# Cached keys gathered already turned, with their rotation partners, instead of rotated in rows and transposed by TensorE

## The chip, the cores and the metric

The kernel runs on one core of a Trainium2 chip. The metric is the device time of one execution in microseconds (us); lower is better. Engines are named as the profile names them: PE is TensorE (PEld its weight loads), DVE is VectorE, ACT is ScalarE, POOL is GpSimd, and SP is SyncE, which here only issues transfers.

## What is computed

The reference is one decoder layer in float32: self-attention over a selected cache, layer norm, cross-attention, layer norm, a linear layer with low-rank experts, layer norm. There are 2048 tokens (32 rows of 64) of 512 features. The change lies in the self-attention alone, which is cut here to what matters:

```python
q = (x @ wq.T).reshape(b, l, 32, 128)           # 32 query heads
k = (x @ wk.T).reshape(b, l, 8, 128)            # 8 key/value groups
v = (x @ wv.T).reshape(b, l, 8, 128)
q, k = apply_rope(q, cos, sin), apply_rope(k, cos, sin)   # one angle per feature pair
k_sel = k_cache[block_idx].reshape(-1, 8, 128)  # 16 blocks of 32 cached keys
v_sel = v_cache[block_idx].reshape(-1, 8, 128)
k_full = concatenate([k_sel, k[0]])             # 512 cached keys and 64 new ones
v_full = concatenate([v_sel, v[0]])
scores = einsum('bhld,bhtd->bhlt', q, repeat(k_full, 4)) / sqrt(128)
out = einsum('bhlt,bhtd->bhld', softmax(scores), repeat(v_full, 4))
return out.reshape(b, l, 4096) @ wo.T
```

All tokens have the same position, so one rotation by one set of angles serves every query and every new key. The kernel never rotates the queries: it applies the inverse rotation to the cached keys instead, and multiplies the new keys by cos^2 + sin^2. A pair of neighbouring features (e, o) of a cached key becomes (e cos + o sin, o cos - e sin).

## The kernel before

**Units.** The self-attention is a loop over 128 units `n`: 8 groups, in each 4 blocks of 512 tokens, in each 4 heads. `r = n % 16` is the place of a unit in its group, `b = n // 4` its block, `h` its head. A unit treats its 512 tokens in four tiles of 128. For each tile PE makes 128x576 scores against `kT` (features on the partitions, 576 keys) into one of two PSUM rooms (`sc`, two buffers); DVE takes the row maximum (L884); ACT does the exponential with the sum (L890); DVE inverts the sum (L919); ACT or DVE scales (L921, L923); DVE turns 32x32 blocks (L931). When all four tiles of a unit are turned, `move` (L943) rearranges them with 16 transfers, issued by SP, into `pT`, and two units later PE multiplies by the values (`values`, L951). For units 0, 1, 2 one quarter of these transfers is issued by POOL instead.

**Queries and projections.** Between the tiles PE computes the queries of the next block and the output projection of a block before, by a seven-product scheme; in blocks 8 to 31 the queries (`qd`, L1170) use a deeper form of it, for which POOL loads operands (L1147, `load_tokens`) and adds up the results (`post`, L1185 to L1191). POOL also makes the sums of weights and tokens for these schemes (`wo_sums` L262 to L265, `outer_sums` L1132, `output_sums` L351 to L355).

**Keys of the next group.** While group `g` runs, the keys of `g + 1` are made ready. `gather_keys` fetches at r = 4 to 7 one quarter of the cached keys each (128 rows of 512 bytes, an indirect transfer, L774), after DVE has made its row numbers (L789); `gather_values` does the same for the values in the same units. From r = 8 on, `rotate` turns the pairs in two halves, with four DVE and two POOL instructions each (L808 to L813); `new_keys` makes the 64 new keys and values on PE at r = 8; `cached_keys` transposes the rotated rows with four PE instructions (L848) into a PSUM bank at r = 10, and two ACT instructions (L851) scale them into `kT`. Group 0 does all that in an opening stage, from rows that arrive early.

**Order.** In the opening stage the order of all five engines is the order of the code (`manual_schedule`). In the loop that holds for PE, DVE, ACT and POOL; SP's order is made by the scheduler, which takes an instruction when what it needs is ready. An engine runs its queue in order, and a waiting instruction holds up all behind it. Loads that can wait are put into a list, `spread`, from which POOL issues one at certain places of a unit.

**Tokens.** The token features of block `b + 2` are loaded in four pieces of 256 KB (`load_pieces`, L122), up to block 7.

Of the kernel before, what the change touches and what calls it, by code (L numbers as in the profile page):

```python
# [28 lines left out]
NKEY = NSEL + SEQ  # L29
# [23 lines left out]
def decoder_layer(  # L53
# [13 lines left out]
    wvT: bass.AP,  # L67
    woT: bass.AP,
    k_cache: bass.AP,
    v_cache: bass.AP,  # L70
    block_idx: bass.AP,
    xwq: bass.AP,
    xbq: bass.AP,
    xwkv: bass.AP,
# [633 lines left out]
    with ExitStack() as ph:  # L708
# [64 lines left out]
        def gather(g, dst, src, t):  # L773
            nc.gpsimd.indirect_dma_start(  # L774
                out=dst[:, t, :], out_offset=None, in_=src,
                in_offset=bass.IndirectOffsetOnAxis(ap=rows_cur[g][:, t : t + 1], axis=0),
            )

        def gather_keys(g, t):
            if t == 0:  # L780
                rows_cur[g] = kv.tile([P, NKT], I32, tag="row", name=f"row{g}")
                kn_cur[g] = kv.tile([P, NKT, HD], F32, tag="kn", name=f"kn{g}", bufs=1)
                kr_cur[g] = kv.tile([P, NKT, HD], F32, tag="kr", name=f"kr{g}", bufs=1)
                vs[g] = kv.tile([P, NKC, HD], F32, tag="v", name=f"v{g}")
            if g == 0:
                if t == 0:
                    nc.vector.tensor_scalar(rows_cur[g], row_f, 0.0, None, ALU.add)
            else:
                nc.vector.tensor_scalar(  # L789
                    rows_cur[g][:, t : t + 1], row_f[:, t : t + 1], float(g), None, ALU.add  # L790
                )
            gather(g, kn_cur[g], k_rows, t)

        def gather_values(g, t):
            gather(g, vs[g], v_rows, t)

        def rotate(g, t0=0, t1=NKT):

# [21 lines left out]
        def new_keys(g):  # L820

            wk, wv = wkv_cur.pop(g)
            kTs[g] = kv.tile([P, NKEY], F32, tag="kT", name=f"kT{g}")
# [41 lines left out]
        def scores(n, i):  # L867
            scores_first(n, i)
            scores_last(n, i)
# [325 lines left out]
        for dst, src in ((cs2, cos2), (sn2, sin2)):  # L1195
            nc.sync.dma_start(out=dst, in_=src)
        nrm2 = kc.tile([P, 1], F32, name="nrm2")
        for dst, src in ((bk, xbk), (bv, xbv)):
            nc.sync.dma_start(out=dst, in_=src)
        load_group(0, nc.sync)  # L1200
# [10 lines left out]
        for i in range(2):  # L1211
# [2 lines left out]
                xTs[0].rearrange("p c (j k) -> p c j k", j=TPB)[:, :, :, : SEQ // TPB],  # L1214
            )
        nc.vector.tensor_tensor(t[1], q[0, 1], q[0, 0], sub)
        nc.vector.tensor_tensor(wq0[7], wq0[1], wq0[5], sub)
        nc.vector.tensor_tensor(wq0[5], wq0[5], wq0[4], ALU.add)
        nc.vector.tensor_tensor(t[2], q[1, 1], t[1], sub)
        nc.vector.tensor_tensor(wq0[6], wq0[5], wq0[1], sub)  # L1220
        rotate(0, 0, NKT // 2)
        nc.vector.tensor_tensor(wq0[3], wq0[2], wq0[6], sub)
        nc.vector.tensor_tensor(nrm2, cs2, cs2, ALU.mult)
        nc.vector.tensor_tensor(sn2, sn2, sn2, ALU.mult)
        nc.vector.tensor_tensor(nrm2, nrm2, sn2, ALU.add)
# [58 lines left out]
        for n in range(N):  # L1284
            b, h = divmod(n, REP)
            g, r = units[n][0], n % PER
            if r == REP + 2 and g + 1 < NKV:
                load_group(g + 1, nc.gpsimd)
            if r in gathers and g + 1 < NKV:
                gather_keys(g + 1, gathers[r])  # L1290
            if 0 < n <= PER:
                b2, j = divmod(n - 1, TPB)
                args = dict(out=acc[b2][:, j, :], in_=rows(x, b2)[:, j, :])
# [116 lines left out]
            if n < (PLAIN - 2) * REP or n >= N - REP:  # L1410
                def leaf(place):
                    for part in leaves.pop(4 * (n - 1) + place, ()):
                        part()
                    if 4 * (n - 1) + place not in full:
                        run_some(spread, 1)

                scores(n, 0)
                step(0)
                leaf(0)
                spare_bank()  # L1420
                run_some(rotations, 1)
                scores(n, 1)
                if n - 1 in short:
                    move(n - 1, (3,), nc.gpsimd)
                if n == N - 1:
                    kv_sums()
                if n >= 2:
                    values(n - 2, 0, first_half)
                leaf(1)
                step(1)  # L1430
                scores(n, 2)
                step(2)
                if h == 1 and b and wo_sums:
# [12 lines left out]
                step(3)  # L1446
                spare_bank()
            else:
                assert not leaves
                k = REP * h  # L1450
                filled = h == 1 and b + 1 >= PLAIN and b + 1 < NB
                scores(n, 0)
                project()
                run_some(rotations, 1)
                scores_first(n, 1, lambda: query(k))
                scores_last(n, 1)
                if n - 1 in short:
                    move(n - 1, (3,), nc.gpsimd)
                if h != REP - 1:
                    values(n - 2, 0, first_half)  # L1460
                    query(k + 1)
                run_some(rotations, 1)
                scores(n, 2)
                if h == REP - 1:
                    query(k + 1)
                if h != 1:
                    project()
                if h == REP - 1:
                    values(n - 2, 0, first_half)
                elif filled:  # L1470
                    query(6)
                spare_bank()
                if r in gathers and g + 1 < NKV:
                    gather_values(g + 1, gathers[r])
                scores_first(n, 3, None if filled else lambda: query(k + 2))
# [794 lines left out]
```

## Time and profile before

| what | value |
|---|---|
| time, median of 3 runs | 2975.94 us (2974.57 to 2977.52) |
| the profiled execution's own time | 2976.36 us |
| its span in the profile | 2974.6 us, so 1.8 us lie around it |
| granted TensorE clock | 0.999 |
| PE busy | 2953.1 us, 99% of the span |
| DVE, ACT, POOL busy | 64%, 50%, 57% |
| DMA engines | six to seven tenths busy in the first half |
| chain that ended last | PE 96%, DVE 2%, DMA 1%, ACT 1% |
| self-attention loop | units start at about 21 us (unit 0), 41 (2), 61 (4), 85 (6), 115 (8), then some 14 us each |

The times of instructions come from one profiled execution on the only core. A busy PE in this profile includes the pipelined ends of its matmuls, so the chain that ended last, which gives each instruction the time by which it moved the end, is the better view for what a PE instruction costs.

### The profile page before, as it was taken

The page shows a single profiled execution, that of the slowest core. Times are in us where ns is not written, and L with a number is a line of the kernel's source. Part 1 is how long each engine was busy: PE and PEld are TensorE (multiplying, and loading weights), DVE is VectorE, ACT ScalarE, POOL GpSimd, SP SyncE. Part 2 cuts the span into 40 slices and gives each one's busy share as a digit, 9 for nine tenths or more (in the row PEclk, how much of TensorE's full clock was granted, in tenths as well). Part 3 has the DMA queues.
Part 4 walks back from the last instruction along what each step waited for, and adds up shares of the span by engine and source line. Part 5 has one row for each costly group of instructions (what it writes and reads, how often), then busy time and mean ns, then how long its engine had stood idle before and what let it go on. Part 6 is the DMA issues. An engine that isn't in the chain of part 4 may idle for free.

```text
span 2974.6 us, 49393 instructions
## 1 busy us (share of the span) xinstructions
PE 2953.1 (99%) x17152; PEld 2336.0 (79%) x17152; DVE 1907.8 (64%) x3569; ACT 1480.7 (50%) x3303; POOL 1699.4 (57%) x1698
## 2 busy tenths in 40 slices
PE   9999999999999999999999999999999999999998
PEld 6677777777777777777777768999999999999965
DVE  6666666666666666666666665636666665666676
ACT  4444455555555455455555552334555555555564
POOL 5666554564564564664663534658577577567532
PEclk9999999999999999999999999999999999999999
DMA  6677656666566666566565554766455545445420
GB/s 170 185 197 194 173 143 157 159 162 158 156 164 155 156 167 158 153 168 155 155 169 154 136 132 148 255 235 214 160 185 184 169 166 194 166 162 184 137 82 36
DMA packets 220262, 487.31 MB, mean 164 GB/s; under 512 B 52912, under 2 KB 87856, under 8 KB 211824
## 3 DMA queue, kind: packets, MB, share of 16 engines
q1 hardware_dynamic: 177872, 341.51, 39.6%
q0 software_dynamic: 40752, 140.94, 16.8%
q8 instruction: 139, 2.28, 0.3%
q10 hardware_dynamic: 1392, 1.70, 0.2%
q14 instruction: 107, 0.88, 0.1%
HBM read 264.27 MB, written 46.66 MB: 105 GB/s over the span
## 4 chain that ended last, share of the span: by engine, by line
PE 96%; DVE 2%; DMA 1%; ACT 1%; SPq 0%; issue 0%; POOL 0%; POOLq 0%; DVEq 0%
PE po L951 17%; PE s L877 17%; PE qd L1170 9%; PE sx L1766 2%; PE pox L1849 2%; PE qx_0x L519 2%; PE qx_1x L519 2%; PE qx_2x L519 2%; PE qx_3x L519 2%; PE wx_3y L380 1%; PE wx_2y L380 1%; PE wx_0y L380 1%; PE w_3y L380 1%; PE w_2y L380 1%; PE w_1y L380 1%; PE w_0y L380 1%
## 5 line engine op out<-in xcount | busy, mean ns | idle before, releaser
L877 PE MATMUL s<-kT,qT 128*128 128x288 f32 x2048 | 581.3, 408 | 0.0
L890 ACT ACTIVATE p<-s,nmax 128x576 f32<-128x576 f32 x512 | 378.3, 739 | 358.6 <-DVE nmax L884 333.7
L951 PE MATMUL po<-pT,v 128*128 128x512 f32 (+1 forms) x1280 | 549.5, 603 | 4.8 <-DMA pT<-T 3.5
L884 DVE TENSOR_REDUCE nmax<-s 128x1 f32<-128x576 f32 x512 | 384.4, 751 | 246.8 <-PE s L877 241.3
L921 ACT ACTIVATE p<-p,den 128x576 f32<-128x576 f32 x416 | 322.7, 776 | 358.7 <-DVE den L919 354.8
L877 PEld LDWEIGHTS s<-kT,qT 128*128 128x128 f32 x2048 | 371.0, 190 | 107.2 <-issue 31.1
L931 DVE STREAM_TRANSPOSE T<-p 128x576 f32<-128x576 f32 x512 | 395.5, 772 | 48.1 <-ACT p L921 40.8
L1147 POOL DMA_DIRECT2D tq<-tq x336 | 182.9, 547 | 416.9 <-PE qd L1170 406.2
L951 PEld LDWEIGHTS po<-pT,v 128*128 128x128 f32 (+1 forms) x1280 | 204.2, 189 | 191.0 <-issue 178.1
L1170 PEld LDWEIGHTS qd<-tq,wq 128*128 128x128 f32 x1344 | 174.5, 191 | 48.4 <-issue 32.3
L1170 PE MATMUL qd<-tq,wq 128*128 128x128 f32 x1344 | 179.0, 276 | 0.0
L1170 PEld LDWEIGHTS qd<-tq,xT 128*128 128x128 f32 x1008 | 136.3, 191 | 51.9 <-issue 23.0
L1170 PE MATMUL qd<-tq,xT 128*128 128x128 f32 x1008 | 142.1, 277 | 0.0
L1869 ACT ACTIVATE oTx<-pox,bv 128x128 f32<-128x128 f32 x248 | 71.3, 490 | 128.6 <-PE pox L1849 128.6
L919 DVE RECIPROCAL den<-den 128x1 f32<-128x1 f32 x512 | 78.4, 153 | 72.1 <-ACT p L890 70.4
L1191 POOL TENSOR_TENSOR qT<-qT,tx 128x512 f32<-128x512 f32 x72 | 89.2, 1265 | 61.7 <-DVE qT L1179 61.6
L351 POOL TENSOR_TENSOR sox<-oTx,oTx 128x512 f32<-128x512 f32 x31 | 39.3, 1268 | 148.5 <-DVE oTx L1871 144.7
L1798 ACT ACTIVATE exps<-exps,denx 128x64 f32<-128x64 f32 x480 | 121.1, 338 | 0.0
L561 POOL TENSOR_TENSOR qTx<-d_in 128x512 f32<-128x512 f32 x68 | 85.3, 1276 | 34.5 <-ACT d_in L537 26.7
L890 ACT ACTIVATION_READ_ACCUMULATOR p<-s,nmax 128x1 f32 x512 | 99.5, 194 | 0.0
L1177 ACT COPY tx<-qd 128x512 f32<-128x512 f32 x96 | 56.1, 584 | 67.8 <-PE qd L1170 62.6
L561 POOL TENSOR_TENSOR qTx<-d 128x512 f32<-128x512 f32 x60 | 75.1, 1274 | 24.6 <-ACT d L537 23.2
(630 smaller groups left out, 6350.5 us busy)
## 6 DMA issues: line engine op xcount, KB each, us to landing
pT<-T SPq DMA_DIRECT2D x1016, 80.0 KB
pT<-T SPq DMA_DIRECT2D x1008, 64.0 KB
xT<-tl SPq DMA_DIRECT2D x28, 1792.0 KB
tq<-tq POOLq DMA_DIRECT2D x168, 256.0 KB
tlb<-tl SPq DMA_DIRECT2D x28, 1344.0 KB
tq<-tq POOLq DMA_DIRECT2D x168, 192.0 KB
kv_room<-kv SPq DMA_DIRECT2D x32, 512.0 KB
pTx<-Tx SPq DMA_DIRECT2D x256, 64.0 KB
```

What stands on the lines that cost most here:

```text
L380: nc.tensor.matmul(self.banks[b][:, m, :], self.left[i][:, k, m * P : (m + 1) * P], self.right[i][:, k, :], start=(first and m + k == 0), ...
L519: nc.tensor.matmul(o[:, j, :], self.left[s][:, j, LEFT[i], :], self.right[s][:, j, RIGHT[i], :], start=(first and j == 0), stop=(j == len( ...
L561: nc.gpsimd.tensor_tensor(self.q[:, :, i, :, v, :], x.rearrange("p (o u) n -> p o u n", o=2), y.rearrange("p (o u) n -> p o u n", o=2), AL ...
L877: nc.tensor.matmul(s[:, a, :HALF], query_block(n, i), kTs[g][:, a * HALF : (a + 1) * HALF], start=True, stop=True,)
L884: nc.vector.tensor_reduce(nmax, s[:, :, :HALF], AX.XY, ALU.max, negate=True)
L890: nc.scalar.activation(p.rearrange("q (a k) -> q a k", a=2), s[:, :, :HALF], AF.Exp, bias=nmax, accum_out=den,)
L921: nc.scalar.activation(p, p, AF.Copy, scale=den)
L931: nc.vector.transpose(Ts[n][:, :, i, :], ps_.pop((n, i)).rearrange("q (b k) -> q b k", k=SQ))
L951: nc.tensor.matmul(pos[n].rearrange("d (a q) -> d a q", a=NQD), vs[units[n][0]][rows, v, :], pTs[n // 2][rows, :, chunk, :], skip_group_ch ...
L1147: nc.gpsimd.dma_start(out=tq[:, r, : 4 - s, :], in_=tq_all[b % NTB][:, r, 4 * s : 4 + 3 * s, :],)
L1170: nc.tensor.matmul(o[:, j, :], wdeep[s][:, j, LEFT[i], :], tq[:, RIGHT[i], j, :], start=(first and j == 0), stop=(j == js - 1), skip_group ...
L1798: nc.scalar.activation(e[:, k, :], e[:, k, :], AF.Copy, scale=den[:, k : k + 1])
```

## The change

Two new inputs are laid out by the host: `k_turned`, the key cache with the features as rows and the 32 keys of a block as columns, each row followed by the row of its rotation partner (64 numbers, 256 bytes), and `blocks`, the 16 block numbers.

For groups 1 to 7 (the second to the eighth), the keys are now fetched from `k_turned`: 16 indirect transfers for each group, one for each block of 32 keys, each with 128 rows (one per feature) of 256 bytes, two in each unit from r = 2 to r = 9. They arrive with the features on the partitions. At r = 10 `rotate_turned` makes `kT` out of them: in each of two steps, two ACT instructions multiply the keys by cos (one number per partition), and two DVE instructions add the partners times plus or minus sin. The transposes on PE, their copies by ACT, and the rotation by DVE and POOL are no longer there for these groups. Group 0 stays as it was.

Once, at the start of unit 1, `turned_setup` makes the constants: a load of the block numbers issued by SP, an index by POOL, and eight DVE instructions on one to sixteen numbers per partition, one of them a sum over 64. The row numbers of a group's keys are made at once at r = 2, those of its values at r = 4.

In the opening, the four DVE instructions that make cos^2 + sin^2 stand earlier, before two sums of weights, and the second half of group 0's rotation stands directly behind the first. The four token pieces are spread over three heads (1, 2, 1) instead of two (2, 2).

```diff
+        def turned_setup():
+            blk_i = kc.tile([P, NBLOCKS], I32, name="blk_i")
+            nc.sync.dma_start(out=blk_i, in_=blocks.partition_broadcast(P))
+            d_i = kc.tile([P, 1], I32, name="d_i")
+            nc.gpsimd.iota(d_i, pattern=[[0, 1]], base=0, channel_multiplier=1)
+            d_f = kc.tile([P, 1], F32, name="d_f")
+            nc.vector.tensor_copy(d_f, d_i)
+            nc.vector.tensor_copy(block_rows, blk_i)
+            nc.vector.tensor_scalar(block_rows, block_rows, float(NKV * HD), d_f, ALU.mult, ALU.add)
+            sign = turn_cs[:, 1:2]
+            even = ident.rearrange("p (j two) -> p j two", two=2)[:, :, 0]
+            nc.vector.tensor_reduce(sign, even, AX.X, ALU.add)
+            nc.vector.tensor_scalar(sign, sign, 2.0, -1.0, ALU.mult, ALU.add)
+            nc.vector.tensor_tensor(sign, sign, sn2, ALU.mult)
+            nc.vector.tensor_scalar(sign, sign, SCALE, None, ALU.mult)
+            nc.vector.tensor_scalar(turn_cs[:, 0:1], cs2, SCALE, None, ALU.mult)
+
+        def gather_turned(g, j):
+            if j == 0:
+                turned_rows[g] = kv.tile([P, NBLOCKS], I32, tag="rowt", name=f"rowt{g}", bufs=1)
+                nc.vector.tensor_scalar(turned_rows[g], block_rows, float(g * HD), None, ALU.add)
+                room = kv.tile([P, 2, NKT, HD], F32, tag="kn", name=f"kn{g}", bufs=1)
+                kn_cur[g] = room.rearrange("p a t (j n) -> p (a t j) n", n=2 * BLOCK)
+            nc.gpsimd.indirect_dma_start(
+                out=kn_cur[g][:, j, :], out_offset=None, in_=k_turned,
+                in_offset=bass.IndirectOffsetOnAxis(ap=turned_rows[g][:, j : j + 1], axis=0),
+            )
+
+        def rotate_turned(g, i):
+            src = kn_cur[g].rearrange("p (t r s) (o k) -> p s t r o k", r=2, s=2, o=2)
+            b0 = (0, SHARED + 1)[i]
+            dst = kTs[g].rearrange("p (s b k) -> p s b k", s=2, k=SQ)[:, :, b0 : b0 + NKT, :]
+            own, other = src[:, :, :, i, 0, :], src[:, :, :, i, 1, :]
+            for s in range(2):
+                nc.scalar.activation(dst[:, s], own[:, s], AF.Copy, scale=turn_cs[:, 0:1])
+            for s in range(2):
+                nc.vector.scalar_tensor_tensor(
+                    dst[:, s], other[:, s], turn_cs[:, 1:2], dst[:, s], ALU.mult, ALU.add
                 )
...
         nc.vector.tensor_tensor(t[1], q[0, 1], q[0, 0], sub)
+        nc.vector.tensor_tensor(nrm2, cs2, cs2, ALU.mult)
+        nc.vector.tensor_tensor(sq2, sn2, sn2, ALU.mult)
+        nc.vector.tensor_tensor(nrm2, nrm2, sq2, ALU.add)
+        nc.vector.tensor_scalar(nrm2, nrm2, SCALE, None, ALU.mult)
...
         rotate(0, 0, NKT // 2)
+        rotate(0, NKT // 2, NKT)
         nc.vector.tensor_tensor(wq0[3], wq0[2], wq0[6], sub)
-        nc.vector.tensor_tensor(nrm2, cs2, cs2, ALU.mult)
-        nc.vector.tensor_tensor(sn2, sn2, sn2, ALU.mult)
-        nc.vector.tensor_tensor(nrm2, nrm2, sn2, ALU.add)
-        nc.vector.tensor_scalar(nrm2, nrm2, SCALE, None, ALU.mult)
...
         new_keys(0)
-        rotate(0, NKT // 2, NKT)
...
-            if r in gathers and g + 1 < NKV:
-                gather_keys(g + 1, gathers[r])
+            if n == 1:
+                turned_setup()
+            turned = 2 * (r - 2) if 2 <= r < 2 + NBLOCKS // 2 and g + 1 < NKV else None
+            if turned is not None:
+                gather_turned(g + 1, turned)
...
-                rotations = [
-                    lambda g=g, t=t: rotate(g + 1, t, t + NKT // 2) for t in (0, NKT // 2)
-                ]
-            if r == 2 * REP + 1 and g + 1 < NKV:
-                later.append(lambda g=g: cached_keys(g + 1))
+                kTs[g + 1] = kv.tile([P, NKEY], F32, tag="kT", name=f"kT{g + 1}")
+            if r == 2 * REP + 2 and g + 1 < NKV:
+                rotations = [lambda g=g, i=i: rotate_turned(g + 1, i) for i in range(2)]
...
-            if b2 < PLAIN and k in (0, 1):
+            if b2 < PLAIN and k in (0, 1, 2):
                 if k == 0:
                     xTs[b2] = token_room(b2, f"xT{b2}")
-                for c in (2 * k, 2 * k + 1):
+                for c in ((0,), (1, 2), (3,))[k]:
...
                 if r in gathers and g + 1 < NKV:
                     gather_values(g + 1, gathers[r])
+                if turned is not None:
+                    gather_turned(g + 1, turned + 1)
```

The last three lines stand in both forms of the unit (with the plain and with the deep queries), behind the unit's third tile of scores. In the deep form, units of head 1 have finished the first half of `post` by then.

More of the change, by code (lines that the diff above doesn't have):

```diff
@@ L69, in decoder_layer @@
     k_cache: bass.AP,
+    k_turned: bass.AP,
     v_cache: bass.AP,
     block_idx: bass.AP,
+    blocks: bass.AP,
     xwq: bass.AP,
@@ L781, in gather_keys @@
                 rows_cur[g] = kv.tile([P, NKT], I32, tag="row", name=f"row{g}")
-                kn_cur[g] = kv.tile([P, NKT, HD], F32, tag="kn", name=f"kn{g}", bufs=1)
-                kr_cur[g] = kv.tile([P, NKT, HD], F32, tag="kr", name=f"kr{g}", bufs=1)
+                room = kv.tile([P, 2, NKT, HD], F32, tag="kn", name=f"kn{g}", bufs=1)
+                kn_cur[g], kr_cur[g] = room[:, 0], room[:, 1]
                 vs[g] = kv.tile([P, NKC, HD], F32, tag="v", name=f"v{g}")
[L785 to L791, printed above, removed]
+                nc.vector.tensor_scalar(rows_cur[g], row_f, 0.0, None, ALU.add)
@@ L792, in gather_keys @@
             gather(g, kn_cur[g], k_rows, t)
         def gather_values(g, t):
+            if t == 0 and g:
+                rows_cur[g] = kv.tile([P, NKT], I32, tag="row", name=f"row{g}")
+                nc.vector.tensor_scalar(rows_cur[g], row_f, float(g), None, ALU.add)
+                vs[g] = kv.tile([P, NKC, HD], F32, tag="v", name=f"v{g}")
             gather(g, vs[g], v_rows, t)
+        NBLOCKS = NSEL // BLOCK
+        block_rows = kc.tile([P, NBLOCKS], F32, name="block_rows")
+        turn_cs = kc.tile([P, 2], F32, name="turn_cs")
@@ new lines, in decoder_layer @@
+        turned_rows = {}
+        def turned_setup():
[14 more added lines that the diff above has]
+            nc.vector.tensor_scalar(turn_cs[:, 0:1], cs2, SCALE, None, ALU.mult)
@@ new lines, in gather_turned @@
+        def gather_turned(g, j):
+            if j == 0:
+                turned_rows[g] = kv.tile([P, NBLOCKS], I32, tag="rowt", name=f"rowt{g}", bufs=1)
+                nc.vector.tensor_scalar(turned_rows[g], block_rows, float(g * HD), None, ALU.add)
+                room = kv.tile([P, 2, NKT, HD], F32, tag="kn", name=f"kn{g}", bufs=1)
+                kn_cur[g] = room.rearrange("p a t (j n) -> p (a t j) n", n=2 * BLOCK)
[3 more added lines that the diff above has]
+            )
@@ new lines, in rotate_turned @@
+        def rotate_turned(g, i):
[8 more added lines that the diff above has]
+                    dst[:, s], other[:, s], turn_cs[:, 1:2], dst[:, s], ALU.mult, ALU.add
+                )
@@ L824, in new_keys @@
             wk, wv = wkv_cur.pop(g)
-            kTs[g] = kv.tile([P, NKEY], F32, tag="kT", name=f"kT{g}")
+            if g == 0:
+                kTs[g] = kv.tile([P, NKEY], F32, tag="kT", name=f"kT{g}")
             new = bank([P, 1, TB], f"new{g}", "po1")[:, 0, :]
@@ L1197, in decoder_layer @@
         nrm2 = kc.tile([P, 1], F32, name="nrm2")
+        sq2 = kc.tile([P, 1], F32, name="sq2")
         for dst, src in ((bk, xbk), (bv, xbv)):
@@ L1474, in decoder_layer @@
                     gather_values(g + 1, gathers[r])
+                if turned is not None:
+                    gather_turned(g + 1, turned + 1)
                 scores_first(n, 3, None if filled else lambda: query(k + 2))
@@ L2225 @@
     feature_major = g["x"].reshape(NTB, P, TPB, DIM).transpose(3, 0, 2, 1).reshape(DIM, NT)
+    keys = g["L0_attn_k_cache"].reshape(NBLK, BLOCK, NKV, HD).transpose(0, 2, 3, 1)
     laid = {
@@ L2240 @@
         "k_cache": g["L0_attn_k_cache"].reshape(NBLK * BLOCK, NKV * HD),
+        "k_turned": np.stack(
+            [keys, keys.reshape(NBLK, NKV, HD // 2, 2, BLOCK)[:, :, :, ::-1].reshape(keys.shape)],
+            axis=3,
+        ).reshape(NBLK * NKV * HD, 2 * BLOCK),
         "v_cache": g["L0_attn_v_cache"].reshape(NBLK * BLOCK, NKV * HD),
         "block_idx": np.repeat(g["L0_attn_block_idx"].reshape(NSEL // P, -1), BLOCK, axis=1).T,
+        "blocks": g["L0_attn_block_idx"],
         "xwq": g["L0_xattn_Wq"],
```

## The prediction

> **What bounds the kernel now.** I read the page's busy times and the end of its chain first, then what PE waits for, then the chain around the transposes that go, then the order of events in the two places where new work enters a queue.
>
> ```profile
> PE 2953.1 (99%) x17152; PEld 2336.0 (79%) x17152; DVE 1907.8 (64%) x3569; ACT 1480.7 (50%) x3303; POOL 1699.4 (57%) x1698
> PE 96%; DVE 2%; DMA 1%; ACT 1%; SPq 0%; issue 0%; POOL 0%; POOLq 0%; DVEq 0%
> ```
>
> PE sets the end. Work taken from DVE, ACT or POOL is worth nothing by itself; work taken from PE is worth its place in the chain, and a new wait of PE is lost in full. The next lines are PE's waits (total us, times, longest), first from 20 to 300 us, then from 300 to 1770:
>
> ```profile
> PE po L951 <- DMA pT<-T: 3.4, 3, 1.5
> PE po L951 <- issue: 0.6, 1, 0.6
> ...
> PE po L951 <- issue: 0.7, 1, 0.7
> PE po L951 <- DMA pT<-T: 0.2, 1, 0.2
> ```
>
> So there are 4.0 us to be won from waits before 300 us, all for the moved probabilities `pT`, and under 1 us later. The chain around the last transposes (start, us by which it moved the end):
>
> ```profile
> 1489.97 1.73 PE w_1x L380 x8
> 1491.70 0.44 PE pkt L848 x4
> 1492.14 0.97 PE s L877 x4
> ```
>
> Four transposes cost the chain 0.44 us, though the group of L848 lists 273 ns for each: they overlap. This row decides the size of the gain.
>
> **What the change removes.** Seven groups times 0.44 us is 3.1 us, all of it on PE's path. The copies by ACT (two of 380 ns a group) and the rotation by DVE and POOL are off the path. The Trainium skill, "TensorE: Matmul & The Clock Gate", Part 4 (PE-mode transpose), gives some 275 ns for one transpose inside a kernel. 28 of them at that price would be an estimate of 7.7 us; the row's duration agrees, the chain does not, and the sum goes by the chain.
>
> **The opening.** The timeline shows DVE idle 0.49 us for a weight transfer before 11.07 us, and the four small sums (L1223 to L1226) at 15.82 to 16.38, ahead of the sums that PE waits for: PE idles 0.84 us before group 0's transposes at 18.89. Their inputs were asked for by 6.3 us. Moved into the idle time, they free 0.56 us of DVE behind it; some is lost where DVE and POOL now rotate side by side. I take -0.4, bounds -0.8 (PE's whole idle time) and 0.
>
> **Unit 1: DVE's setup.** These lines are from the timeline; the bracket is idle time and what ended it.
>
> ```profile
> 33.00 0.78 DVE L931 STREAM_TRANSPOSE T<-p 128x576 f32<-128x576 f32 x1 [0.84 <-ACT p L921]
> 33.70 0.72 DVE L884 TENSOR_REDUCE nmax<-s 128x1 f32<-128x576 f32 x1
> 36.14 1.28 POOL L262 TENSOR_TENSOR wo<-wo,wo 128x512 f32<-128x512 f32 x1
> 41.13 0.76 DVE L884 TENSOR_REDUCE nmax<-s 128x1 f32<-128x576 f32 x1 [0.27 <-PE s L877]
> 44.86 1.98 POOL L943 DMA_DIRECT2D pT<-T  x4 [3.38 <-DVE T L931]
> 46.13 0.86 PEld L877 LDWEIGHTS s<-kT,qT 128*128 128x128 f32 x4 [0.49 <-ACT p L890]
> 54.38 2.81 PE L951 MATMUL po<-pT,v 128*128 128x512 f32 x6 [0.58 <-issue]
> ```
>
> The eight instructions come between the first two lines. Small ones here take 0.15 to 0.17 us (L1223 to L1226, L749 to L752), so 1.3 us. Behind them wait the unit's first maximum, its exponential, and then PE for the room that this frees. DVE catches up only 0.27 us (the idle time at 41.13), and at 46.13 the loads of PE already wait for ACT. So 1.0 us reaches PE; bounds 0 (hidden) and 1.4.
>
> **Unit 2: POOL's first turned gather.** It stands at the start of unit 2, waits for DVE's row numbers, and those stand behind the last turn of unit 1 (43.79, 0.78). Today the four `wo` sums run from 36.14 to 41.5, while POOL would idle; they stand behind that gather in the code, so they start at about 45 + 1.3, end 5.3 us later, and only then POOL issues its quarter of unit 1's moves: at about 51.6 instead of 44.86, done by 53.6, landing some 2 us later at 55.6. PE takes `pT` at 54.38, or about 55.4 with the delay above: SP's own 12 transfers allow no sooner. The later landing, with that delay in it too, is 1.0 us on, near 56.1 to 56.6. I take +0.7, bounds 0 and 2.0.
>
> **The token pieces and the early DMA load.** At 77.13 and 90.88 PE waits 1.44 and 1.49 us for `pT`. SP's waits from 60 to 92 us name the cause:
>
> ```profile
> SPq L943 <- DMA pT<-T: 4.7, 6, 1.2
> ```
>
> SP waits for its own earlier moves, which share the DMA engines with what POOL loads (DMA share 0.76 from 65 to 70, 1.05 from 80 to 85). The piece that leaves unit 4 for unit 5 is 256 KB, some 1.2 us at the 214 GB/s seen there; unit 5 passes one to unit 6 and stays as it was. So the first wait loses 0.9, the second nothing. Bounds -1.4 and +0.5 (the gathers are 256-byte rows).
>
> **84 more gathers.** 112 turned ones stand for 28. A gather takes POOL 1.00 us (L774, 128 rows) and 0.30 before the next, so 109 us in 1275 us of idle time. Where POOL has none is at the end of blocks that load the next group's weights:
>
> ```profile
> 604.75 0.55 POOL L1115 DMA_DIRECT2D wq<-in_wqD  x1
> 611.37 1.26 POOL L1132 TENSOR_TENSOR wq<-wq,xT 128x512 f32<-128x512 f32 x1 [4.30 <-DMA wq<-in_wqD]
> 617.40 3.73 POOL L1191 TENSOR_TENSOR qT<-qT,tx 128x512 f32<-128x512 f32 x3
> 621.72 0.78 PEld L877 LDWEIGHTS s<-kT,qT 128*128 128x128 f32 x4 [0.76 <-POOL qT L1191]
> ```
>
> PE's next block needs the first of the three sums (L1191), done at 618.7: 3.0 us of slack. (In block 17 the scores at 953.44 begin before the third sum ends at 953.85, so the first is enough.) The last of the 16 gathers, at r = 9 behind `post`, enters this stretch: 1.3 us later, no wait. The other gathers of r = 8 and 9 lie in idle time (5.2 us before 578.48), and those before them too. The Trainium skill, "DMA: Bandwidth & Descriptors", table at its head, asks for at least 512 bytes a piece for full rate, and these have 256; its bandwidth table gives 0.95 us of DMA time for 64 KB, so 84 more at that price are, as an estimate, 80 us spread over some 800: no other sum. No run here shows a 256-byte gather.
>
> **The rotation at r = 10.** ACT gains four instructions of 128x128 (between 338 ns, L1798, and 490, L1869; I take 0.4) and loses two of 0.38; DVE has four of some 0.3 (L810) for eight. DVE now waits for ACT, which waits for the last gather; behind them stand the next maximum and exponential. PE has a second room, so about 3 us pass before it waits. I take 0, bounds 0 and 0.5 a group.
>
> **Sum.** -3.1 - 0.4 + 1.0 + 0.7 - 0.9 = -2.7 us, so 2973.7 against the profiled execution's 2976.36. That one is 0.4 above the median of the runs, so 2973.2 there. A measurement of this kernel can tell about 0.2%, 6 us, from no change: this lies within it.
>
> **Rival 1, slower: DVE waits for the block numbers.** The second setup instruction needs SP's load. If SP issues it where the code has it, behind unit 0's moves (from 33.81, twelve at 0.63, to 41.4, and 2.05 us to land, as the first block numbers took), DVE resumes at 43.5 instead of 33.8 and PE loses 9.7 us more: 2982.9. It decides from a wait of 2.7 us (slower at all), or 8.7 (by over 0.2%). For it: a wait in DVE's queue is paid in full here. Against: SP's order is the scheduler's, and today it issues the token pieces of units 1 and 2 before unit 0's moves:
>
> ```profile
> 20.09 1.78 SPq L122 DMA_DIRECT2D xT<-in_xT  x4
> 33.81 0.61 SPq L943 DMA_DIRECT2D pT<-T  x1
> ```
>
> **Rival 2: the gathers or the rotation reach PE in the loop.** If POOL is late by 3.8 us instead of 1.3 in the five blocks shown above, that is 5 x 0.8 = 4.0; if the rotation costs its upper bound, 7 x 0.5 = 3.5. Either gives about 2977, up to 2981 with both. Against: POOL's idle time in r = 8 and 9.
>
> **Rival 3, faster: the early waits vanish.** Gathers that wait for no row of their own unit let POOL load earlier. All 4.0 us of waits gone, the opening at its best, no new delay: -3.1 - 0.8 - 4.0 = -7.9, 2968.0. Against: the DMA engines are full from 80 to 87 us, and no bytes leave unit 5.
>
> **How the numbers follow.** Forecast 0.62, rival 1 0.11, rival 2 0.16 (of it 0.04 beyond 0.2%), rival 3 0.11. The forecast's bounds are -3.1 - 0.8 - 1.4 = -5.3 and -3.1 + 1.4 + 2.0 + 0.5 = +0.8; most of rival 2 lies up to 2979.5. A range of 2969.8 to 2979.5 leaves out rival 1, the end of rival 2 and rival 3. Faster by over 0.2% (under 2970.0): 0.11. Slower (over 2981.9): 0.11 + 0.04 = 0.15. Within: 0.74.
>
> **What would show it.** L848 with four instructions left; PE's chain in a deep group shorter by 0.44 us, and no wait of PE from 300 to 1770 beyond today's. At the start: the eight small DVE instructions after 33.7 without idle time among them (idle: rival 1), PE's wait for `pT` near 56 longer than 0.58, the one near 77 shorter than 1.44. The first sum of L1191 nearer than 1 us to PE's next scores, or PE idle behind it, is rival 2. The forecast is wrong if the units of a deep group last longer than now.

## The result, and the profile after

The changed kernel takes 2997.44 us (median of 6 runs, 2995.57 to 3002.01), against 2976.30 us of the kernel before (6 runs, 2974.30 to 2980.67): ratio 1.0073, 95% interval 1.0060 to 1.0086. It is slower by 21 us, where 3 us less was predicted, and lies outside the range. The profiled execution took 2995.57 us, its span 2993.8, at a granted clock of 0.997 (before: 2976.36, 2974.6, 0.999).

The page's busy times and the end of its chain, after:

```profile
PE 2959.4 (99%) x17124; PEld 2338.7 (78%) x17124; DVE 1918.4 (64%) x3535; ACT 1486.3 (50%) x3317; POOL 1773.7 (59%) x1755
PE 93%; DVE 2%; DMA 1%; issue 1%; ACT 1%; SPq 1%; POOL 1%; POOLq 0%; DVEq 0%; ACTq 0%
```

28 matmul instructions are gone (17152 to 17124), as the change says, and yet PE's share of the chain fell from 96 to 93 per cent: PE waits more. Its waits over the whole span (total us, times, longest):

```profile
PE qd L1219 <- ACT qT L1226: 10.8, 5, 2.2
PE q_0x L382 <- DMA xT<-in_xT: 5.2, 1, 5.2
PE po L1000 <- DMA pT<-T: 4.4, 4, 2.5
PE q_0z L382 <- DVE wq L1272: 3.0, 1, 3.0
```

The first line is new: five waits of 2.2 us for the copy of the queries, one in each of groups 2 to 6 (counted from 0) at r = 10, where the rotation now stands. The last one was 0.4 us before. The other two have forerunners (5.1, and 3.5 in four, of which the longest was 1.5).

**The wait at r = 10.** The timeline around one of them (start, us, bracket: idle time before it and what ended it):

```profile
824.36 1.02 POOL L827 DMA_INDIRECT kn<-in_k_turned,rowt  x1
824.64 3.51 DVE L841 SCALAR_TENSOR_TENSOR kT<-kn,turn_cs,kT 128x128 f32<-128x128 f32 x2
825.39 1.28 POOL L353 TENSOR_TENSOR so<-oT,oT 128x512 f32<-128x512 f32 x1
826.75 1.26 POOL L354 TENSOR_TENSOR so<-so,oT 128x512 f32<-128x512 f32 x1
828.08 0.15 DVE L968 RECIPROCAL den<-den 128x1 f32<-128x1 f32 x1
828.33 0.78 ACT L970 ACTIVATE p<-p,den 128x576 f32<-128x576 f32 x1 [3.70 <-DVE den L968]
829.01 0.46 ACT L1226 COPY qT<-qd 128x384 f32<-128x384 f32 x1
829.52 1.48 PE L1219 MATMUL qd<-tq,xT 128*128 128x128 f32 x6 [2.16 <-ACT qT L1226]
831.85 0.64 DVE L841 SCALAR_TENSOR_TENSOR kT<-kn,turn_cs,kT 128x128 f32<-128x128 f32 x2 [1.15 <-ACT kT L839]
```

Read it from below. The two adds of the rotation's second step, at 831.85, take 0.64 us together. The same two of the first step, at 824.64, take 3.51, and end when POOL's sums L353 and L354 have ended. Behind them on DVE stands the inverse of the sum (L968); ACT stands idle 3.70 us for that, with the copy of the queries (L1226) behind it in its queue; PE needs that copy. Nothing in the chain is long but the two adds.

**The clock behind it.** The windows view of the same place (stretch, length, busy time and instructions of PE, PEld, DVE, ACT, POOL, then the granted clock, the DMA share and GB/s):

```profile
828.00:830.00 2.00, 0.48 (x3) 0.48 (x4) 2.00 (x5) 1.67 (x3) 2.00 (x3) 0.93 0.47 115
830.00:832.00 2.00, 2.00 (x8) 1.71 (x8) 0.85 (x3) 1.17 (x5) 2.00 (x4) 0.50 0.58 134
832.00:834.00 2.00, 2.00 (x7) 1.53 (x7) 1.60 (x5) 1.13 (x3) 1.15 (x3) 0.71 0.84 256
834.00:836.00 2.00, 2.00 (x12) 1.70 (x11) 1.33 (x4) 0.92 (x3) 0.00 (x0) 1.00 0.93 297
```

After the wait the granted clock falls to 0.50 for some 3 us: the six matmuls above last 1.48 us. Behind the first of the five waits (group 2, 606 to 610 us) it stayed at 1.00, the six took 0.94 us, and there the group lost 2.0 us net of its transposes; behind the other four it fell, and they lost 3.6 to 3.7 us each.

**The opening.** Timeline after:

```profile
5.09 0.33 SPq L1245 DMA_DIRECT2D cs<-in_cos  x1
5.77 0.33 SPq L1245 DMA_DIRECT2D sn<-in_sin  x1
11.78 0.16 DVE L1267 TENSOR_TENSOR nrm<-cs 128x1 f32<-128x1 f32 x1 [1.89 <-DMA cs<-in_cos]
12.59 0.16 DVE L1268 TENSOR_TENSOR sq<-sn 128x1 f32<-128x1 f32 x1 [0.65 <-DMA sn<-in_sin]
13.78 0.69 DVE L1272 TENSOR_TENSOR wq<-wq 128x512 f32<-128x512 f32 x1
14.53 3.38 PE L382 MATMUL q_0z<-tx,wq 128*128 128x256 f32 x8 [3.00 <-DVE wq L1272]
```

The small sums that were moved forward wait in DVE's queue for one number per partition, asked for at 5.09 and 5.77 and there only at about 11.8 and 12.6. The weight sums stand behind them, and PE behind those, for 3.00 us. Before the change the same product stood so:

```profile
12.54 1.99 PE L380 MATMUL q_0z<-tx,wq 128*128 128x256 f32 x8 [0.45 <-DVE wq L1218]
```

Its eight matmuls now take 3.38 us, because the granted clock is 0.50 from 14 to 16 us. So a part of what the opening loses is the clock. In a later run with the same order (`e1_psum`) a wait of 3.4 us there was followed by a clock of 1.00, and the first scores came 1.1 us later than before instead of 2.3.

**Unit 3.** Timeline after:

```profile
47.90 1.02 POOL L827 DMA_INDIRECT kn<-in_k_turned,rowt  x1 [9.43 <-DVE rowt L824]
53.00 1.28 POOL L267 TENSOR_TENSOR wo<-wo,wo 128x512 f32<-128x512 f32 x1
54.21 2.02 POOL L992 DMA_DIRECT2D pT<-T  x4
59.33 2.81 PE L1000 MATMUL po<-pT,v 128*128 128x512 f32 x6 [2.53 <-DMA pT<-T]
```

POOL idles 9.43 us for the row numbers, then makes the `wo` sums, and only then issues its quarter of unit 1's moves: PE waits 2.53 us for `pT` instead of 0.58.

Comparing the starts of the units in the two traces gives each step of the prediction its size:

| step | predicted, us | found, us |
|---|---|---|
| opening, up to unit 0 | -0.4 | +2.3 |
| DVE's setup, units 1 and 2 | +1.0 | +0.7 |
| first gather ahead of the `wo` sums, unit 3 | +0.7 | +1.95 |
| waits for `pT` near 77 and 91 us | -0.9 | -2.4 |
| transposes, 7 groups | -3.1 | -3.1 |
| 84 more gathers | 0 | 0 |
| rotation at r = 10 | 0 | +19.8 |
| sum | -2.7 | +19.3 (spans: +19.2) |

The rotation's row is what these units lost, with 0.44 us for the transposes added back in each group. The +19.8 are 1.1 us in group 1, where one add took 1.35 us, and 18.7 in groups 2 to 6.

### The profile page after: what moved, and what is told of

It reads as the page before. It is cut to its first block, busy times and chain, and to the rows that moved or that the text cites. A ratio compares the mean times of both kernels' runs of the same rounds, so it can differ in the third digit from the quotient of the medians.

```text
span 2993.8 us, 49409 instructions
## 1 busy us (share of the span) xinstructions
PE 2959.4 (99%) x17124; PEld 2338.7 (78%) x17124; DVE 1918.4 (64%) x3535; ACT 1486.3 (50%) x3317; POOL 1773.7 (59%) x1755
## 2 busy tenths in 40 slices
DMA packets 223095, 489.16 MB, mean 163 GB/s; under 512 B 54400, under 2 KB 89344, under 8 KB 214656
## 4 chain that ended last, share of the span: by engine, by line
PE 93%; DVE 2%; DMA 1%; issue 1%; ACT 1%; SPq 1%; POOL 1%; POOLq 0%; DVEq 0%; ACTq 0%
PE po L1000 16%; PE s L926 16%; PE qd L1219 9%; PE sx L1821 2%; PE pox L1904 2%; PE qx_0x L521 2%; PE qx_1x L521 2%; PE qx_2x L521 2%; PE qx_3x L521 2%; PE wx_3y L382 1%; PE wx_2y L382 1%; PE wx_0y L382 1%; PE w_3y L382 1%; PE w_0y L382 1%; PE w_2y L382 1%; PE wx_1y L382 1%
## 5 line engine op out<-in xcount | busy, mean ns | idle before, releaser
L1196 POOL DMA_DIRECT2D tq<-tq x336 | 186.1, 558 | 400.4 <-PE qd L1219 391.2
L827 POOL DMA_INDIRECT kn<-in_k_turned,rowt x112 | 111.4, 994 | 41.7 <-issue 30.0
L968 DVE RECIPROCAL den<-den 128x1 f32<-128x1 f32 x512 | 78.8, 154 | 77.8 <-ACT p L939 69.3
L353 POOL TENSOR_TENSOR sox<-oTx,oTx 128x512 f32<-128x512 f32 x31 | 39.4, 1271 | 148.3 <-DVE oTx L1926 144.5
L1226 ACT COPY tx<-qd 128x512 f32<-128x512 f32 x96 | 56.3, 586 | 71.6 <-PE qd L1219 71.6
```

What stands on the lines that cost most here:

```text
L827: nc.gpsimd.indirect_dma_start(out=kn_cur[g][:, j, :], out_offset=None, in_=k_turned, in_offset=bass.IndirectOffsetOnAxis(ap=turned_rows[g ...
L1196: nc.gpsimd.dma_start(out=tq[:, r, : 4 - s, :], in_=tq_all[b % NTB][:, r, 4 * s : 4 + 3 * s, :],)
```

## Experiments

Theory: an add of the rotation, which reads two operands from SBUF, is held while POOL runs an instruction that reads SBUF, and all else follows through DVE's and ACT's queues. Rivals: the gathers, ACT's new work, the place at r = 10 itself, or the form of the add (it reads and writes the same place).

**Without the adds.** `e3_no_add` leaves the adds out, so that the cached keys are not rotated:

```diff
-            for s in range(2):
-                nc.vector.scalar_tensor_tensor(
-                    dst[:, s], other[:, s], turn_cs[:, 1:2], dst[:, s], ALU.mult, ALU.add
-                )
```

> DVE's four adds of each group are left out, so the cached keys of groups 1 to 7 are not rotated, only scaled by cos; gathers and ACT's instructions stay. Shared access: PE's waits for ACT's query copies (10.8 us, 5 times) are gone, 2976 to 2977. Rivals gathers and ACT: both causes are still there, 2995 to 2998.

One run: 2977.42 us, span 2975.1, no wait for the copy of the queries at all. The gathers and ACT's instructions are all there, at the same places: by themselves they do not cost the 20 us.

**One operand in PSUM.** `e1_psum` lets ACT write its product to a free PSUM bank:

```diff
+            room = bank([P, NKT, P], f"pkt{g}_{i}", "po1")
+            part = [room[:, s, :].rearrange("p (t k) -> p t k", k=SQ) for s in range(2)]
-                nc.scalar.activation(dst[:, s], own[:, s], AF.Copy, scale=turn_cs[:, 0:1])
+                nc.scalar.activation(part[s], own[:, s], AF.Copy, scale=turn_cs[:, 0:1])
-                    dst[:, s], other[:, s], turn_cs[:, 1:2], dst[:, s], ALU.mult, ALU.add
+                    dst[:, s], other[:, s], turn_cs[:, 1:2], part[s], ALU.mult, ALU.add
```

> The cosine product goes to PSUM instead of kT, so that DVE's add reads one operand from SBUF and one from PSUM; place, counts and gathers stay. Theory 'shared access' (DVE's add with two SBUF operands is held while POOL's sums run): the adds of step one in groups 2 to 6 take 0.35 to 0.5 us instead of 2.18 and 1.40, PE no longer waits there, some 4.1 us in each of five groups return: 2977 us (ratio to before 1.000). Rival 'gathers' (84 more gathers make POOL late, and the sums behind them) and rival 'ACT' (four more ACT instructions hold up the copies of the queries): no change, 2997.

2977.44 us (10 runs, 2974.54 to 2979.58; before 2976.93), ratio 1.0004, interval 0.9994 to 1.0013. Its timeline at the same place:

```profile
820.65 1.01 POOL L827 DMA_INDIRECT kn<-in_k_turned,rowt  x1 [0.15 <-issue]
821.04 0.60 DVE L843 SCALAR_TENSOR_TENSOR kT<-kn,turn_cs,pkt 128x128 f32<-128x128 f32 x2
821.68 1.29 POOL L353 TENSOR_TENSOR so<-oT,oT 128x512 f32<-128x512 f32 x1
```

The adds run beside the gather in 0.60 us, as soon as they are issued. Those of the second step run beside one of POOL's sums, just as fast:

```profile
825.51 1.27 POOL L357 TENSOR_TENSOR so<-oT,so 128x512 f32<-128x512 f32 x1
825.55 0.60 DVE L843 SCALAR_TENSOR_TENSOR kT<-kn,turn_cs,pkt 128x128 f32<-128x128 f32 x2 [1.36 <-ACT pkt L841]
```

The wait of PE is gone, and some 20 us come back.

**Two operands in SBUF, but not in place.** That version changes two things: the operand's memory, and that the add no longer overwrites what it reads. `e11_apart` changes the second alone, with a tile in SBUF:

```diff
+            room = kv.tile([P, 2, P], F32, tag="part", name=f"part{g}_{i}", bufs=1)
```

(the other lines as above).

> The changed kernel, with the cosine product in a tile of its own in SBUF instead of in kT, so that DVE's add no longer reads and writes the same place, but still has two SBUF inputs. Theory (two SBUF inputs against POOL's sums): nothing changes; the first adds of groups 2 to 6 take 2.18 and 1.40 us as before, PE waits 2.2 us for the copy of the queries five times, and the time stays near 2997. Rival (it is the in-place form that is slow, and the PSUM version was fast because it was not in place): all adds take 0.35 us, no such wait, 2977.

2997.74 us (4 runs, 2996.63 to 2999.94; before 2976.25), ratio 1.0071, interval 1.0055 to 1.0086. The adds' group (least, median and longest ns) and the first of the two steps:

```profile
L843 DVE SCALAR_TENSOR_TENSOR kT<-kn,turn_cs,part x28: 341/353/2172, 154.5 to 1512.8; 128x128 f32<-128x128 f32 x28
```

```profile
829.72 3.50 DVE L843 SCALAR_TENSOR_TENSOR kT<-kn,turn_cs,part 128x128 f32<-128x128 f32 x2
834.58 0.94 PE L1221 MATMUL qd<-tq,xT 128*128 128x128 f32 x6 [2.15 <-ACT qT L1228]
```

As slow as in place, so overwriting plays no part. What the held add has and the free one has not is that both operands come from SBUF. The Trainium skill, "SBUF — State Buffer", section "Who interferes with whom", states this: "A DVE instruction with two SBUF inputs contends with a GpSimd instruction that reads SBUF"; it calls the pair of ports that the two engines share an exclusive lock. These runs agree: 0.35 us became 2.18 and 1.40 us, and with one operand in PSUM the longest was 0.35. I had not weighed that page against this step.

**The last gather earlier.** `e4_gather_first` issues both gathers of r = 9 at the start of that unit, so that POOL's sums come closer behind it; the rotation stays at r = 10.

```diff
+                if r == 2 * REP + 1:
+                    gather_turned(g + 1, turned + 1)
-                if turned is not None:
+                if turned is not None and r != 2 * REP + 1:
```

> The last of a group's 16 gathers is issued at the start of r = 9 instead of behind the first half of post, so it no longer stands ahead of the output sums; the rotation stays at r = 10. Shared access: the first add now waits only for the rest of one sum (some 1.3 us instead of 2.18), the second for the next (1.4): about 1 us of 4.1 returns in each of five groups, 2992. Rival gathers: the late gather is what costs, so all of it returns, 2977. Rival ACT: 2997.

2985.62 us (6 runs, 2981.55 to 2987.69), ratio 1.0029, interval 1.0016 to 1.0041: some 12 us came back, more than twice what I expected. In the two traces it is 1.2 us in group 2 and 2.9 in each of groups 3 to 6. The timeline in group 3:

```profile
821.74 1.27 POOL L353 TENSOR_TENSOR so<-oT,oT 128x512 f32<-128x512 f32 x1
822.23 2.27 DVE L841 SCALAR_TENSOR_TENSOR kT<-kn,turn_cs,kT 128x128 f32<-128x128 f32 x2
823.08 1.27 POOL L354 TENSOR_TENSOR so<-so,oT 128x512 f32<-128x512 f32 x1
825.86 0.94 PE L1219 MATMUL qd<-tq,xT 128*128 128x128 f32 x6 [0.92 <-ACT qT L1226]
```

The adds are held for 2.27 us instead of 3.51, so PE waits 0.92 instead of 2.16, and its six matmuls then take 0.94: the clock stays at 1.00 (window 826 to 828 us). I had counted only the shorter wait. The traced run is one of the two fastest of the six (2981.85); whether the clock fell in the slower ones is not known.

**Another place.** `e2_r12` moves the rotation two units on, where I took POOL to run no sums.

```diff
-            if r == 2 * REP + 2 and g + 1 < NKV:
+            if r == 3 * REP and g + 1 < NKV:
```

> The rotation runs at r = 12 instead of 10, where POOL has no output sums; nothing else moves. Shared access: adds 0.35 us, about 20 us return, 2977. Rival gathers: POOL is late as before, 2997. Rival ACT: the same four instructions stand in another unit and cost there what they cost here, 2997.

2998.43 us (4 runs, 2991.45 to 3006.48), ratio 1.0080, interval 1.0057 to 1.0102. The expectation missed, because its premise was wrong: at r = 12 POOL makes the weight sums of the next queries.

```profile
851.84 4.14 DVE L841 SCALAR_TENSOR_TENSOR kT<-kn,turn_cs,kT 128x128 f32<-128x128 f32 x2
853.31 1.30 POOL L1117 TENSOR_TENSOR wq<-wq 128x512 f32<-128x512 f32 x1
854.54 1.28 POOL L1187 TENSOR_TENSOR xT<-xT 128x512 f32<-128x512 f32 x1
```

The adds are held beside other sums just as well, and PE waits there (4 times, 7.7 us in all). So the miss speaks for the theory: it is not the place, nor one certain POOL instruction.

**The opening.** From here on each kernel keeps the operand in PSUM. `e5_nrm_back` puts the four small sums back behind `wq0[3]`:

```diff
-        nc.vector.tensor_tensor(nrm2, cs2, cs2, ALU.mult)
...
         nc.vector.tensor_tensor(wq0[3], wq0[2], wq0[6], sub)
+        nc.vector.tensor_tensor(nrm2, cs2, cs2, ALU.mult)
...
```

> Cosine product in PSUM as in the first experiment, and the four small sums back behind the third sum of weights, where they stood before; the second half of the rotation stays forward. Theory 'late loads' (the four sums hold DVE until the one-number-per-partition loads of cos and sin land): PE's wait for the weight sum before its third product falls from some 3 us to under 0.5, and the first scores come 2 to 3 us sooner than with the change. 2975. Rival 'order' (bringing forward the rotation is what holds DVE): the wait stays at 3 us, 2977.5.

2975.80 us (10 runs, 2973.02 to 2977.50; before 2975.90), ratio 0.9996, interval 0.9987 to 1.0005. In its profile the wait for `q_0z` is gone, and the first scores come 0.6 us earlier than before, where `e1_psum` had them 1.1 later and the change 2.3. So the moved sums were what held the opening. I had expected 2 to 3 us; the median, against its own before, moved by only 0.6 us from `e1_psum`. The profiled run shows one reason, a longer loss in unit 3:

```profile
56.68 5.46 PE L1002 MATMUL po<-pT,v 128*128 128x512 f32 x6 [2.79 <-DMA pT<-T]
```

```profile
56.00:58.00 2.00, 1.32 (x2) 0.83 (x3) 1.70 (x4) 1.61 (x4) 2.00 (x4) 0.50 0.67 193
```

After this wait of 2.79 us the clock is 0.50 until about 62 us, and the same six matmuls take 5.46 us instead of 2.81 in the changed kernel. How many of the other runs met that, no trace shows.

**Unit 3.** `e6_wo_first` also lets POOL begin the `wo` sums of unit 2 before the first gather.

```diff
+            if n == 2:
+                wo_sums.pop()()
             turned = 2 * (r - 2) if 2 <= r < 2 + NBLOCKS // 2 and g + 1 < NKV else None
...
-            if n == 2:
-                wo_sums.pop()()
```

> As the one before, and the sums of the output weights stand ahead of the first turned gather in POOL's queue. If that order is what makes unit 1's quarter of the moves late, PE's longest wait for pT near 59 us falls from 2.5 us to 0.6, and 1.9 us return: 2973. If DVE's setup or SP is the cause, the wait stays and the time is 2975.

2972.19 us (11 runs, 2970.51 to 2974.09), ratio 0.9984, interval 0.9975 to 0.9993. POOL's queue in unit 2 is now

```profile
45.94 1.03 POOL L827 DMA_INDIRECT kn<-in_k_turned,rowt  x1 [4.06 <-DVE rowt L824]
46.96 2.00 POOL L994 DMA_DIRECT2D pT<-T  x4
```

so the moves go out at 46.96 instead of 54.21, and the wait for `pT` near 55 us is 0.33.

**DVE's setup.** `e7_split` also moves the five instructions that make the factors of the rotation from unit 1 to unit 6:

```diff
             nc.vector.tensor_scalar(block_rows, block_rows, float(NKV * HD), d_f, ALU.mult, ALU.add)
+
+        def turn_factors():
             sign = turn_cs[:, 1:2]
...
+            if n == 6:
+                turn_factors()
```

> As the one before, and the five setup instructions that make the factors of the rotation stand at unit 6 instead of 1; the three for the row numbers stay. If DVE's setup costs PE what the two units after it lost (0.45 and 0.21 us), half of it returns: 2972.7. If it was hidden, 2973.

2971.82 us (11 runs, 2969.89 to 2975.38), ratio 0.9988, interval 0.9979 to 0.9997. In its trace the losses of units 1 and 2 (0.21 and 0.45 us) are gone; between this version and the one before the times can't tell. It is faster than both kernels: by 4 us than the one before, and by some 25 than the changed one, each set against its own before.

**The token pieces and the early waits.** Two runs put them back to 2 and 2: `e8_pieces22` on top of `e1_psum`, `e10_split22` on top of `e7_split`.

```diff
-            if b2 < PLAIN and k in (0, 1, 2):
+            if b2 < PLAIN and k in (0, 1):
-                for c in ((0,), (1, 2), (3,))[k]:
+                for c in (2 * k, 2 * k + 1):
```

> Cosine product in PSUM, four sums as in the change, and the token pieces over two heads as before. If the spreading of the pieces is what shortens PE's early waits for pT (units 5 and 6 gain 1.5 and 0.6 to 0.9 us against before), these gains are gone, up to 2.4 us; if it is the gathers that no longer wait for a row of their own unit, they stay.

One run, 2980.78 us: no wait for `pT` near 77 us or near 90, as with 1, 2, 1. I first read from this that the pieces do nothing. But in that run unit 4 began some 9 us later than in the kernel before, with waits of 4.2 us in the opening and 2.80 in unit 3, and a PE that comes late may find its transfers landed. So it was tried again in the version without these delays:

> The best version so far with the four token pieces over two heads, 2 and 2, as before the change. If the spreading is worth nothing: 2971.8, units 5 and 6 start as early as with 1, 2, 1. If it is worth what my prediction gave it: 0.9 us more, 2972.7, with PE's wait for pT near 77 us longer by that.

2973.95 us (11 runs, 2972.36 to 2975.73; before 2976.25), ratio 0.9992, interval 0.9983 to 1.0001. Beside it `e9_rows` keeps the pieces at 1, 2, 1, but makes group 1's row numbers two at a time in each unit, so that the first gather of a unit waits for DVE again:

```diff
+            if g == 1 and j % 2 == 0:
+                nc.vector.tensor_scalar(
+                    turned_rows[g][:, j : j + 2], block_rows[:, j : j + 2], float(g * HD), None, ALU.add
+                )
```

> The best version so far (product in PSUM, small sums back, first sum of wo ahead of the gather, factors at unit 6), with the row numbers of group 1 made two at a time by DVE at the start of each unit 2 to 9, as the old gathers had it, so that POOL's first gather of a unit waits for DVE again. Theory (the early pT waits became shorter because POOL no longer waits for a DVE row of the same unit): PE's wait for pT in units 4 and 5 comes back to some 1.4 us, and the time rises by 1.5 to 2.4 us to about 2974. Rival (they became shorter for another reason, such as the smaller gathers or the transposes' absence): the waits stay under 0.5 us, and the time stays within 0.5 us of 2971.8.

2971.98 us (11 runs, 2970.03 to 2974.48), ratio 0.9985, interval 0.9976 to 0.9994. The waits for `pT` between 60 and 100 us in the three traces, pieces back first, then rows back, then `e7_split`:

```profile
76.88 2.84 PE L1004 MATMUL po<-pT,v 128*128 128x512 f32 x6 [1.00 <-DMA pT<-T]
```

```profile
88.22 1.96 PE L1009 MATMUL po<-pT,v 128*128 128x512 f32 x4 [1.23 <-DMA pT<-T]
```

```profile
87.48 1.96 PE L1004 MATMUL po<-pT,v 128*128 128x512 f32 x4 [0.25 <-DMA pT<-T]
```

Each edit brings back one wait: the pieces the one near 77 us (1.00 us; 1.44 before the change), the rows the later one (1.23; 1.49 before the change, at 90.88). For the time that is worth less. From unit 0 to unit 11 the traces lose only 0.3 us with the pieces back and 0.6 with the rows back, since a wait in one unit shortens the next. Later, near 316 us, PE waits for `pT` once more, 1.68 us with the pieces back and 2.09 with the rows back, against 0.43 in `e7_split`; whether the edits bring that is not shown. The edit of the rows also does more than bring back the old order: beside POOL's sums the instruction that makes two row numbers takes 1.00 to 1.24 us, four times in eight, instead of 0.13, while the old one, with a single number, took 0.14 at most. The medians, each against its own before, give 1.8 us for the pieces and nothing for the rows; intervals as wide as 0.0018 (5 us) can't settle such sizes, and that stays open.

## Why the prediction was wrong

**The step that failed is "The rotation at r = 10 ... I take 0, bounds 0 and 0.5 a group."** It was +19.8 us in all, up to 4.1 in a group. Three things were wrong in it. The add was priced by the nearest rotation row, some 0.3 us; 17 of the 28 took about that, the other 11 were held. What POOL runs at that place, the output sums (L351 to L355 of the kernel before), was in the trace, and the prediction did not look at it:

```profile
597.58 1.27 POOL L351 TENSOR_TENSOR so<-oT,oT 128x512 f32<-128x512 f32 x1
598.93 1.27 POOL L352 TENSOR_TENSOR so<-so,oT 128x512 f32<-128x512 f32 x1
```

That trace even had the price of such a hold, in another DVE instruction, the scaling L923. It takes 0.52 us by itself; begun beside a gather, it ended 0.3 us after the sum behind that gather:

```profile
84.53 0.52 DVE L923 TENSOR_SCALAR p<-p,den 128x576 f32<-128x576 f32 x1
99.71 1.03 POOL L774 DMA_INDIRECT v<-in_v_cache,row  x1 [0.30 <-issue]
100.12 2.24 DVE L923 TENSOR_SCALAR p<-p,den 128x576 f32<-128x576 f32 x1
100.76 1.28 POOL L1096 TENSOR_TENSOR tq<-tq 128x512 f32<-128x512 f32 x1
```

Then "PE has a second room, so about 3 us pass before it waits" looked at the scores alone; the wait came at the queries, whose copy stands in ACT's queue behind a scaling that waits for DVE. And the upper bound took the work for its own length; a held instruction costs what holds it, and in four cases of five another 1.65 us for the clock. Rival 2 had the right place, but its price came from the same 0.5. The bound should have been the time from the first add to the end of the POOL sums that can stand beside the two adds, 3.4 us in a group, less the slack, and the clock on top: 2.4 us were lost in the group where the clock stayed, up to 4.1 where it fell.

**The opening (-0.4, found +2.3)** is the second failed step. "Their inputs were asked for by 6.3 us" was read as if they were there. The trace of before had no reader that waited for them, so their landing could not be seen; the gap into which the sums were to fall ended at 11.07, and the inputs landed at 11.8 and 12.6. The clock behind PE's wait, which the prediction did not count either, made it longer. The bound "0" should have been the time that the sums would wait, and rival 1's rule, that a wait in DVE's queue is paid in full, applied here instead.

**Mis-sized:** the gather ahead of the `wo` sums (+0.7, found +1.95, just inside the upper bound of 2.0): the mechanism was as told, with POOL's moves at 54.2 instead of the 51.6 that I had worked out, 2.6 us later, most of it the opening's 2.3. DVE's setup (+1.0, found +0.7), confirmed by its going when the factors moved. The early waits (-0.9, found -2.4): the pieces do take some 1.0 us off the first wait (`e10_split22`), but "the second nothing" was wrong; rival 3 had named the cause for which `e9_rows` speaks, gathers that wait for no row of their own unit, though that edit's slower row numbers may have a share in it. How much of the -2.4 in the changed kernel is only its own lateness of 5 us at that point was not told apart.

**Right:** the transposes: in the trace of `e3_no_add` the unit at r = 10 is 0.44 us shorter in all seven groups. The gathers: 112 at 0.99 us on POOL, and no wait of PE for L1191's successors. Their estimate of 80 us of DMA time took 64 KB for each, but 128 rows of 256 bytes are 32 KB; the bytes that the profiles count agree with that (489.16 MB, against 487.31 before). It did not enter the sum. Rival 1 did not happen: SP issued the load of the block numbers at 14.10, ahead of unit 0's moves, and DVE ran its setup from 36.04 to 37.17 without idle time.

## What to carry to other kernels

Before moving work onto DVE, list what POOL runs at that moment: if the new instruction reads two operands from SBUF, charge it the rest of POOL's sum and of the next one (up to 3.60 us for one add here), then follow the queues behind it, or put one operand into PSUM, which here took back 20 us with two new lines and two changed ones. Look in the trace of before for DVE instructions of one shape whose times differ: they show what such a hold costs. A wait is to be priced with the clock that follows it. And an input that was asked for early has not landed: where no instruction of the trace waits for it, its landing is unknown, and nothing that matters should be queued behind its first reader.

## What was not expected of the hardware

- The hold lasts beyond one instruction. In the changed kernel the first add began 0.29 us after a gather's start and was released only when the output sum behind that gather had ended (2.18 us in all). The two adds at 831.85, beside two transfers that POOL issued (L1196), took 0.64 us together. But the longest add of all, 3.60 us at 852.4 us in `e2_r12`, began beside such a transfer too, and lasted through the two sums behind it. Why one was held and the others not is open.
- Instructions that read one tensor from SBUF are held too, some of them: the scaling L923 and the two row numbers of `e9_rows` above. The turns of 32x32 blocks (L931), which also read one, took 0.77 to 0.78 us in all 512 cases. What sets them apart was not tested.
- The length of PE's wait alone doesn't set the clock. In all traces together, and leaving out the first wait of a run, eight of eleven waits of 2.1 to 2.2 us came with a clock of 0.50, none of three of 2.5 to 2.6 (`e1_psum`, `e3_no_add`, the change, all in unit 3), four of six of 2.7 to 2.9, two of five of 2.9 to 3.5, and all three above 4. Those below 2 us did not. What decides is not shown. The Trainium skill, "TensorE: Matmul & The Clock Gate", section "Why this matters for your kernels", warns of gaps over some 3 us between bursts of matmuls; here shorter ones were enough, while one of 3.4 (`e1_psum`) had no such effect; the measurement decides.
- Two loads of one number per partition took 6.7 and 6.8 us from issue to the instruction that they released, with the DMA engines full in the first part of it (DMA share 1.09 from 6 to 9 us, 0.49 from 9 to 12).
